# The opening of an S4-gated LoRA feed-forward kernel put in another order: adapter loads, adapter products, normalisation and the first chain

## Chip, core, metric

The kernel runs on one core of one Trainium2 chip. The metric is the device time in microseconds of one launch. Three runs of the kernel before took 466.06, 466.60 and 467.17 us, so its median is 466.6 us. Everything is float32.

## The reference, cut to what matters

```python
x  = u                                   # (2, 1024, 512): 2048 tokens of 512
xn = layernorm(x)                        # (x - mean) / sqrt(var + 1e-5), no gain, no bias
s  = fft_convolution(xn, K) + D * xn     # K: an S4 kernel of length 512, along the last axis
def lora(x, w, a, b):                    # rank 16, scaling 2
    return x @ w.T + 2.0 * (x @ a.T) @ b.T
h1 = lora(xn, w1, A1, B1)                # 512 -> 1376
h3 = lora(xn, w3, A3, B3)
f  = lora(silu(h1) * h3, w2, A2, B2)     # 1376 -> 512
out = x + s * silu(f)
```

The inputs w1 and w3 are 1376 x 512 each. 1376 is ten chunks of 128 and a last chunk of 96.

## The kernel before, in words

**Tiling.** The 2048 tokens are four blocks of 512 (b = 0 to 3), each held as four tiles of 128 tokens (`x_in[b][tt]`). A block is loaded (`load_x`), its mean and variance are taken (`norm_stats` on VectorE, or `act_sums`, `act_means`, `act_squares`, `act_variances` on ScalarE and GpSimd), the inverse root is found on VectorE by an integer guess and Newton steps (`norm_root`, `newton_rsqrt`), the tiles are scaled and shifted (`normalize`), turned by TensorE (`transpose`, 16 small matmuls per block) and copied from PSUM by ScalarE into `xr` (and `b12` for the odd blocks).

**Merging the adapters.** A weight tile gets its adapter added before use: TensorE forms B A into a PSUM bank (`lora_product`, 16 rows deep) and VectorE adds twice that to the tile (`merge`, L374). `merge_pair(c, w, half)` does so for one half of the 512 inputs of both w1 and w3 for a pair of chunks c; `lora_last` and `merge_last` do so for the chunk of 96. The adapter factors lie in two tiles, `lo_d` (A1, A3) and `lo_h` (B1, B3); their columns are in two halves, cut at 768 of 1376, and `load_lora(factors, queue, (half,))` loads one half with four transfers. Half 1 holds the last chunk, half 0 the first six chunks.

**Products.** The large product is a two-level Winograd scheme: sums of tokens (`outer_token_sum`, then `inner_token_sum`) and of weights (`outer_weight_sums`, `inner_weight_sum`) on VectorE, seven products per level on TensorE. One `Chain` is seven steps named 1, 2, 6, 7, 5, 3, 4 that go into PSUM banks x, w and y. After step 1 ScalarE copies x to w (L747); after steps 6 and 5 it saves x (`snapshot`, L729); sums with y (`total`, L733) are made on VectorE, gating is on ScalarE and GpSimd. The chain of the last chunk (`last_chain`) works at the outer level alone with four passes a step; each pair of chunks has seven chains (`pair_chain`) with two passes a step. The text calls step 1 of the last chunk "last P1", and so on.

**Order.** The order within TensorE, VectorE, ScalarE and GpSimd is written out by hand. Code that runs straight through comes first; then a heap of events, `at(place, what)`, is emptied in order of place, and each engine works through its own part in that order. Places are labels of order, not times. SyncE (SP) issues nearly all loads in program order; ScalarE's queue issues the adapter loads at the start. Eight semaphores go round among all loads of both queues, so a ninth load is issued only when an older one has landed.

**The opening.** SP loads block 0 (four transfers of 256 KB), block 1, the last chunk (`load_last`), pair 0 (`load_pair`), blocks 2 and 3, and pair 1. TensorE runs 24 idle matmuls on `ident` (`keep_warm`, two passes each), `lora_last`, then between more idle ones the transposes of block 0, and last P1. The two weight halves of pair 0 are merged at the places -9 and -3.8, the statistics of block 2 are taken from place -6 on, and the token sums of blocks 0 and 1 begin at place -2.3.

```python
    at(-9, lambda: merge_pair(0, w_pair[0], 0))
    at(-3.8, lambda: merge_pair(0, w_pair[0], 1))
    for i in range(2):
        at(-6 + i, lambda i=i: transpose(1, range(2 * i, 2 * i + 2), "y"))
    for tt in range(NTT):
        at(-6 + 0.8 * tt, lambda tt=tt: norm_stats(2, (tt,)))
```

Of the kernel before, what the change touches and what calls it, by code (L numbers as in the profile page):

```python
# [34 lines left out]

A_AT = {1: 0, 2: 1, 3: 6, 4: 2, 5: 3, 6: 4, 7: 5}
# [5 lines left out]

def newton_rsqrt(nc, pool, v, shape):

    y = pool.tile(shape, F32, tag="rs_y", name="rs_y")
    t = pool.tile(shape, F32, tag="rs_t", name="rs_t")
    nc.vector.tensor_scalar(
        y.bitcast(I32), v.bitcast(I32), -0.5, float(0x5F3759DF), ALU.mult, ALU.add  # L50
    )
    for _ in range(3):
        nc.vector.tensor_tensor(t, y, y, ALU.mult)
        nc.vector.scalar_tensor_tensor(t, t, -0.5, v, ALU.mult, ALU.mult)
        nc.vector.scalar_tensor_tensor(y, t, 1.5, y, ALU.add, ALU.mult)
    return y
# [40 lines left out]
def s4_gated_ffn(  # L97
# [106 lines left out]
    def after(delay, what):  # L204
        at(now[0] + delay, what)
# [4 lines left out]
    def load_x(b):  # L210
        room = (None, None, t_in[4], t_in[6])[b]
        tiles = []
        for tt in range(NTT):
            t = value() if room is None else room[:, tt, :]
            nc.sync.dma_start(out=t, in_=x[bass.ds(b * TB + tt * P, P), :])
            tiles.append(t)
        return tiles
# [17 lines left out]
    def act_sums(b, tt):  # L235
        if tt == 0:
# [5 lines left out]
    def act_means(b):  # L242
        sums = sums_of_x[b]
        nc.gpsimd.tensor_scalar(sums[:, 1, :], sums[:, 0, :], -1.0 / DIM, None, mult)
        nc.gpsimd.tensor_scalar(norms[b][:, :, 0], sums[:, 0, :], 1.0 / DIM, None, mult)

# [9 lines left out]

    def act_variances(b):
        nc.gpsimd.tensor_scalar(
            norms[b][:, :, 1], sums_of_x[b][:, 2, :], 1.0 / DIM, None, mult
        )  # L260

    def norm_root(mv, *blocks):
        n = len(blocks) * NTT
        veps = small.tile([P, n], F32, tag="veps", name="veps")
        nc.vector.tensor_scalar(veps, mv[:, :, 1], EPS, None, add)
        rstd = newton_rsqrt(nc, small, veps, [P, n])
        shift = small.tile([P, n], F32, tag="shift", name="shift")
        nc.vector.scalar_tensor_tensor(shift, mv[:, :, 0], -1.0, rstd, mult, mult)
# [3 lines left out]
    def normalize(b, on_act=(0, 2)):  # L272
        rstd, shift = norms[b]
        for tt, t in enumerate(x_in[b]):
            one = slice(tt, tt + 1)
            if tt in on_act:
                nc.scalar.activation(
                    t, t, AF.Identity, bias=shift[:, one], scale=rstd[:, one]
                )
            else:  # L280
                nc.gpsimd.tensor_scalar(t, t, rstd[:, one], shift[:, one], mult, add)

# [18 lines left out]
    def outer_token_sum(sb, name):  # L301
        b11, b21, b22 = (xr[:, i, sb] for i in range(3))
        t = [xt[:, i, sb] for i in range(4)]
        one, other = {
            1: (b12[sb], b11),
            2: (t[2], b11),
            3: (b22, b12[sb]),
            4: (b21, t[1]),
        }[name]
        nc.vector.tensor_tensor(t[name - 1], one, other, add if name == 2 else sub)  # L310

# [65 lines left out]
    def load_pair(c):  # L377
        w = wpool.tile([P, 8, 2, 2, P], F32, tag="w", name="w")
        for v, src in enumerate((w1T, w3T)):
            for half in range(2):  # L380
                slot = (1, 2, 0, 3)[2 * v + half]
                rows = src[half * HALF : (half + 1) * HALF, 2 * c * P : 2 * (c + 1) * P]
# [6 lines left out]
    def merge_pair(c, w, half, tag="aux"):  # L389

        ps = [bank(tag), bank(tag)]
        for k in range(2):
            for v in range(2):
                n = slice(k * 2 * P, (k + 1) * 2 * P)
                lora_product(ps[v][:, n], v, 2 * half + k, 2 * c * P, 2 * P, k == 0)
        for v in range(2):
            to = w[:, (1, 2, 0, 3)[2 * v + half]].rearrange("p k m h -> p (k m h)")
            after(1.6 + v, lambda to=to, v=v: merge(to, ps[v]))

# [66 lines left out]
    def load_w2():  # L466
        lora_tiles()
        load_lora(((b2T, a2),), nc.sync, (0, 1))
        w2["a"] = wpool.tile([P, 8, DIM], F32, tag="w", name="w2_a")
        w2["b"] = const.tile([P, 3, DIM], F32, tag="w2b", name="w2_b")  # L470
        nc.sync.dma_start(
            out=w2["a"], in_=w2T[: 8 * P, :].rearrange("(c p) d -> p c d", p=P)
        )
        nc.sync.dma_start(
            out=w2["b"][:, :2], in_=w2T[8 * P : LAST * P, :].rearrange("(c p) d -> p c d", p=P)
        )
        nc.sync.dma_start(out=w2["b"][:LASTR, 2], in_=w2T[LAST * P :, :])
# [4 lines left out]
    def merge_down(*chunks):  # L482

        made = []
        for fc in chunks:
            rows = P if fc < LAST else LASTR
            ps = aux()[:rows, :]
            d, h = lora_factors(0, 1, fc * P, rows)
            nc.tensor.matmul(ps, lhsT=h, rhs=d, start=True, stop=True)  # L489
# [216 lines left out]

    def product(ps, pairs, first):
        for i, (lhsT, rhs) in enumerate(pairs):
            nc.tensor.matmul(  # L709
                ps,  # L710
                lhsT=lhsT,
                rhs=rhs,
                start=first and i == 0,
                stop=i == len(pairs) - 1,
                skip_group_check=True,
            )


    class Chain:

        def __init__(self, pairs, rows, keep, got, late=0):
            self.pairs, self.rows, self.keep, self.got = pairs, rows, keep, got
            self.late = late

# [9 lines left out]
        def step(self, i):  # L736
# [6 lines left out]
            to = self.w if i == 2 else self.y if i in (7, 4) else self.x  # L743
            product(to, self.pairs(i), i in (1, 7))
            if i == 1:
# [47 lines left out]
    def last_chain(ab, sb):  # L793
# [12 lines left out]

        return Chain(pairs, LASTR, lambda o: value(), got, 1)

# [104 lines left out]
    lora_tiles()  # L913
    factors = (a1, b1T), (a3, b3T)
    load_lora(factors, nc.scalar, (1,))
    nc.scalar.activation(warm, warm, AF.Silu)
    load_lora(factors, nc.scalar, (0,))
    x_in[1] = load_x(1)
# [3 lines left out]
    x_in[2], x_in[3] = load_x(2), load_x(3)  # L922
    w_pair[1] = load_pair(1)

    def keep_warm(ps, n, first=False):
# [11 lines left out]
    for ps in primed:  # L937
        keep_warm(ps, 12, True)
    ps_last = lora_last()
    mv = norm_tile(0)  # L940
    norm_stats(0, range(NTT))
    norm_root(mv, 0)
    normalize(0)

    for i in range(2):
        keep_warm(primed[1], (5, 2)[i])
        transpose(0, range(2 * i, 2 * i + 2))
    keep_warm(primed[1], 4)
    mv = norm_tile(1)
    norm_stats(1, range(2))  # L950
    merge_last(w_last, ps_last, 0)
    norm_stats(1, range(2, NTT))
    norm_root(mv, 1)
    merge_last(w_last, ps_last, 1)
    mv_late = norm_tile(2, 3)
# [13 lines left out]
    for c in range(NPAIR):  # L969
# [6 lines left out]
        lambda: last_chain(ab_last, 0),  # L976
        ((1, -11), (2, -8), (7, -2), (6, 1.6), (5, 5.6), (3, 8.6), (4, 11.6)),
    )
    add_chain(
        0,  # L980
        pair_chain(0, 0),
        ((1, -4), (2, -1.8), (7, 3.6), (6, 4.6), (5, 7.6), (3, 10.6), (4, 13.6)),
    )
# [4 lines left out]
    for c in range(1, NPAIR):  # L988
        for n in range(7):

            hurry = (c, n) in ((NPAIR - 2, 6), (NPAIR - 1, 4))
            add_chain(2 + 7 * c + n, pair_chain(c, n), SOON if hurry else PLACES)
    at(-10, lambda: normalize(1))
    at(-9.9, lambda: last_sums(w_last, s_last))
    at(-9, lambda: merge_pair(0, w_pair[0], 0))
    at(-3.8, lambda: merge_pair(0, w_pair[0], 1))
    for i in range(2):
        at(-6 + i, lambda i=i: transpose(1, range(2 * i, 2 * i + 2), "y"))
    for n, name in enumerate((3, 2, 1)):
# [469 lines left out]
```

## Time and profile before

| | before |
|---|---|
| median of three runs | 466.6 us (466.06 to 467.17) |
| the profiled execution, its own time | 465.92 us |
| span of its profile, first to last instruction | 464.1 us |
| granted TensorE clock over the span | 1.00 |
| TensorE busy | 451.9 us, 97% of the span, 1682 matmuls |
| VectorE busy | 290.3 us, 63% |
| ScalarE busy | 136.3 us, 29% |
| GpSimd busy | 194.4 us, 42% |
| DMA | 53.36 MB, 115 GB/s on average |

The profiled execution's own time is 1.8 us above its span; what lies around the span is not shown by the profile. All times below are from the start of the span. A float32 matmul is recorded as two passes, a transpose as one. In the timeline, a row gives the start, the length, the engine, the line, the operation, what is written from what, and in brackets the idle time ahead of it with what ended it. "SPq" and "ACTq" are the queues from which SyncE and ScalarE issue transfers.

### The profile page before, as it was taken

The numbers are of one execution on the slowest core, as the hardware profiler recorded it, in microseconds if no ns is written. First come the engines' busy times: TensorE is split into PE (matmuls) and PEld (weight loads), VectorE is DVE, ScalarE is ACT, GpSimd is POOL, SyncE is SP. The second block draws the span as 40 slices with busy tenths as digits, with TensorE's granted clock in tenths as the row PEclk, the third lists the DMA queues.
The fourth block names the chain that finished last, engine by engine and source line by source line (L and its number), as shares of the span: only waits on it lengthen the run. The fifth ranks groups of instructions, "written<-read, shape, count | busy, mean of one in ns | idle before, by whom it ended". The sixth has DMA issues, their size and how long they took to land.

```text
span 464.1 us, 5003 instructions
## 1 busy us (share of the span) xinstructions
PE 451.9 (97%) x1682; PEld 274.9 (59%) x1682; DVE 290.3 (63%) x494; ACT 136.3 (29%) x281; POOL 194.4 (42%) x156
## 2 busy tenths in 40 slices
PE   8999898989999999999999999999999999999996
PEld 8635333334433443344333344888889898999895
DVE  5898979664776477547745586959786123442222
ACT  2675242433234334432442133111111101111110
POOL 2324262497559555945693359500000112222221
PEclk9999999999999999999999999999999999999999
DMA  8910312015102410241036229296901842422211
GB/s 249 359 43 18 130 57 84 0 54 174 46 23 69 137 45 23 69 151 44 23 98 220 80 83 269 91 333 214 347 1 47 287 139 91 137 90 92 80 57 45
DMA packets 35049, 53.36 MB, mean 115 GB/s; under 512 B 4528, under 2 KB 21168, under 8 KB 34896
## 3 DMA queue, kind: packets, MB, share of 16 engines
q1 hardware_dynamic: 34768, 52.74, 34.6%
q10 hardware_dynamic: 256, 0.31, 0.2%
q8 instruction: 13, 0.21, 0.2%
q14 instruction: 12, 0.10, 0.1%
HBM read 33.64 MB, written 19.40 MB: 114 GB/s over the span
## 4 chain that ended last, share of the span: by engine, by line
PE 83%; DVE 8%; DMA 3%; ACT 2%; POOL 2%; issue 1%; SPq 0%; POOLq 0%
PE x L709 39%; PE y L709 21%; PE w L709 11%; PE aux L881 6%; PE aux L364 2%; PE aux L489 2%; DMA room<-g_dram 2%; DVE s L419 1%; DMA s<-in_x_dram 1%; DVE xt L310 1%; DVE s L733 1%; DVE w L407 1%; DVE t_in L326 1%; POOL s L790 1%; PE w L881 1%
## 5 line engine op out<-in xcount | busy, mean ns | idle before, releaser
L1236 POOL TENSOR_TENSOR o<-o,xin 128x512 f32<-128x512 f32 (+1 forms) x17 | 22.5, 1324 | 140.1 <-DVE o L1235 140.1
L790 POOL TENSOR_TENSOR s<-c,s 128x512 f32<-128x512 f32 (+1 forms) x44 | 59.6, 1356 | 23.2 <-ACT c L782 20.7
L729 ACT COPY s<-x 128x512 f32<-128x512 f32 (+1 forms) x54 | 31.6, 586 | 95.4 <-PE x L709 95.2
L709 PE MATMUL x<-t_in,s 128*128 128x512 f32 (+1 forms) x148 | 56.5, 504 | 0.0
L733 DVE TENSOR_TENSOR s<-s,y 128x512 f32<-128x512 f32 (+1 forms) x54 | 36.5, 681 | 24.1 <-PE y L709 14.4
L823 POOL TENSOR_TENSOR ua_three<-ua_three,s 128x512 f32<-128x512 f32 x20 | 29.8, 1489 | 34.9 <-DVE s L733 34.9
L709 PEld LDWEIGHTS x<-t_in,s 128*128 128x128 f32 x148 | 26.4, 189 | 21.8 <-issue 13.8
L823 POOL TENSOR_TENSOR s<-ua_three,s 128x512 f32<-128x512 f32 x18 | 29.8, 1653 | 21.5 <-DVE s L733 21.5
L709 PE MATMUL y<-t_in,s 128*128 128x256 f32 (+1 forms) x108 | 36.2, 461 | 1.4 <-DVE s L733 1.4
L1257 ACT COPY z<-x 128x256 f32<-128x256 f32 x24 | 8.9, 373 | 83.5 <-PE x L709 83.5
L782 ACT ACTIVATE c<-c 128x512 f32<-128x512 f32 x40 | 25.1, 632 | 12.7 <-DVE c L823 12.7
L709 PEld LDWEIGHTS y<-t_in,s 128*128 128x128 f32 x108 | 20.0, 190 | 13.4 <-issue 8.5
L823 POOL TENSOR_TENSOR s<-u_three,s 128x512 f32<-128x512 f32 x20 | 26.6, 1332 | 0.8
L747 ACT COPY w<-x 128x512 f32<-128x512 f32 (+1 forms) x37 | 21.5, 581 | 8.5 <-PE x L709 8.5
L881 PE MATMUL aux<-conv,xr 128*128 128x128 f32 (+1 forms) x128 | 23.2, 314 | 0.0
L709 PE MATMUL x<-xt,w 128*128 128x512 f32 x40 | 21.0, 607 | 0.7 <-ACT w L747 0.7
L709 PE MATMUL x<-t_in,w 128*128 128x512 f32 x40 | 21.3, 613 | 0.4 <-ACT w L747 0.4
L823 POOL TENSOR_TENSOR u_three<-ua_three,u_three 128x512 f32<-128x512 f32 x10 | 13.3, 1326 | 19.8 <-DVE u_three L733 17.9
L709 PE MATMUL x<-xr,w 128*128 128x512 f32 x40 | 20.8, 615 | 0.6 <-ACT ua_three L729 0.5
L1234 DVE TENSOR_TENSOR aux<-aux,m 128x256 f32<-128x256 f32 x16 | 6.9, 431 | 23.1 <-PE aux L881 23.1
L709 PE MATMUL x<-xr,s 128*128 128x512 f32 x40 | 20.6, 614 | 0.7 <-ACT s L729 0.7
L709 PE MATMUL y<-xt,w 128*128 128x512 f32 x40 | 19.9, 595 | 1.4 <-DVE s L733 1.4
(271 smaller groups left out, 871.5 us busy)
## 6 DMA issues: line engine op xcount, KB each, us to landing
g_dram<-s SPq DMA_DIRECT2D x40, 256.0 KB, 2.1
g<-g_dram SPq DMA_DIRECT2D x10, 512.0 KB, 5.7
xin<-in_x_dram SPq DMA_DIRECT2D x16, 256.0 KB, 2.7
out_dram<-o SPq DMA_DIRECT2D x14, 256.0 KB, 2.0
t_in<-g_dram SPq DMA_DIRECT2D x6, 512.0 KB, 4.2
w<-in_w1T_dram SPq DMA_DIRECT2D x10, 256.0 KB, 3.6
w<-in_w3T_dram SPq DMA_DIRECT2D x10, 256.0 KB, 4.4
s<-in_x_dram SPq DMA_DIRECT2D x8, 256.0 KB, 4.2
```

The lines of the kernel that those rows point to most:

```text
L364: nc.tensor.matmul(ps, lhsT=d[:, dc * P : (dc + 1) * P], rhs=h, start=start, stop=True, skip_group_check=True,)
L489: nc.tensor.matmul(ps, lhsT=h, rhs=d, start=True, stop=True)
L709: nc.tensor.matmul(ps, lhsT=lhsT, rhs=rhs, start=first and i == 0, stop=i == len(pairs) - 1, skip_group_check=True,)
L729: nc.scalar.copy(t, self.x)
L733: nc.vector.tensor_tensor(t, t, self.y, add)
L747: nc.scalar.copy(self.w, self.x)
L782: nc.scalar.activation(c, c if src is None else src, AF.Silu)
L790: nc.gpsimd.tensor_tensor(g, act, g, mult)
L823: (nc.vector if o < 20 else nc.gpsimd).tensor_tensor(to, a, b, add)
L881: nc.tensor.matmul(to, lhsT=x_, rhs=by, start=start, stop=True, skip_group_check=True)
L1236: (nc.vector if last else nc.gpsimd).tensor_tensor(o, o, self.xin[h][:, cols], add)
L1257: nc.scalar.copy(t, xb)
```

## The change

It has these parts:

1. ScalarE runs its first activation (the table load) ahead of the adapter loads instead of between them; adapter half 0 moves from ScalarE's queue to the end of SP's, behind pair 1. The chunks of the weights are walked in another order (`PAIR_AT`: columns 768, 1024, 0, 256, 512), so that pairs 0 and 1 need half 1, which is the half loaded first.
2. The adapter products of pair 0's first half are made right behind `lora_last`, ahead of block 0's transposes; 12 idle matmuls instead of 24 stand in front, 4 instead of 11 around the transposes.
3. Tile 1 of block 0 has its statistics on ScalarE and GpSimd (`act_tile`). The root takes ten instructions of VectorE, `veps` and `shift` among them, instead of twelve. Tile 0 of block 0 is normalised on VectorE instead of ScalarE.
4. Last P1 of blocks 0 and 1 is made in two halves of 256 tokens.
5. The places of the opening move: both halves of pair 0 are merged, and pair 0's chain 1 has its steps 1 and 2, ahead of or between block 1's transposes; the statistics of block 2 move from before the token sums to between and behind them; two of the four squares of block 3 move behind a snapshot.
6. The outer token sums are made in two instructions of 128x512 instead of one of 128x1024.
7. Blocks 2 and 3 are loaded with four transfers of 512 KB instead of eight of 256 KB; w2 is loaded with one transfer more.

```diff
+PAIR_AT = [2 * P * ((c + 3) % NPAIR) for c in range(NPAIR)]
+CHUNK_AT = [PAIR_AT[fc // 2] + fc % 2 * P for fc in range(LAST)] + [LAST * P]
...
-def newton_rsqrt(nc, pool, v, shape):
+def rsqrt(nc, pool, v, shape):
...
-    for _ in range(3):
-        nc.vector.tensor_tensor(t, y, y, ALU.mult)
-        nc.vector.scalar_tensor_tensor(t, t, -0.5, v, ALU.mult, ALU.mult)
-        nc.vector.scalar_tensor_tensor(y, t, 1.5, y, ALU.add, ALU.mult)
+    nc.vector.tensor_tensor(t, y, y, ALU.mult)
+    nc.vector.scalar_tensor_tensor(t, t, -c2, v, ALU.mult, ALU.mult)
+    nc.vector.scalar_tensor_tensor(y, t, c2 * 2.38924456, y, ALU.add, ALU.mult)
+    nc.vector.tensor_tensor(t, y, y, ALU.mult)
+    nc.vector.scalar_tensor_tensor(t, t, 1.0 / part**2, v, ALU.mult, ALU.mult)
+    nc.vector.scalar_tensor_tensor(t, t, -10.0 / 3.0, t, ALU.add, ALU.mult)
+    nc.vector.scalar_tensor_tensor(y, t, 5.0, y, ALU.add, ALU.mult)
...
+    def act_tile(b, tt):
+        one = slice(tt, tt + 1)
+        act_sums(b, tt)
+        act_means(b, one)
+        act_squares(b, tt)
+        act_variances(b, one)
...
-        nc.vector.tensor_tensor(t[name - 1], one, other, add if name == 2 else sub)
+        for k in range(2):
+            to, a, b = (v[:, k] for v in (t[name - 1], one, other))
+            nc.vector.tensor_tensor(to, a, b, add if name == 2 else sub)
...
-            product(to, self.pairs(i), i in (1, 7))
+            product(to, self.pairs(i), i in (1, 7), self.parts if i == 1 else 1)
...
+    nc.scalar.activation(warm, warm, AF.Silu)
     load_lora(factors, nc.scalar, (1,))
-    nc.scalar.activation(warm, warm, AF.Silu)
-    load_lora(factors, nc.scalar, (0,))
...
     w_pair[1] = load_pair(1)
+    load_lora(factors, nc.sync, (0,))
...
     for ps in primed:
-        keep_warm(ps, 12, True)
+        keep_warm(ps, 6, True)
     ps_last = lora_last()
+    merge_pair(0, w_pair[0], 0, ("x", "w"), (-10.6, -10.5))
     mv = norm_tile(0)
-    norm_stats(0, range(NTT))
+    act_tile(0, 1)
+    norm_stats(0, (0, 2, 3))
     norm_root(mv, 0)
-    normalize(0)
-
-    for i in range(2):
-        keep_warm(primed[1], (5, 2)[i])
-        transpose(0, range(2 * i, 2 * i + 2))
+    mv = norm_tile(1)
+    normalize(0, (2,), (0,))
     keep_warm(primed[1], 4)
-    mv = norm_tile(1)
+    transpose(0, range(NTT))
     norm_stats(1, range(2))
     merge_last(w_last, ps_last, 0)
     norm_stats(1, range(2, NTT))
-    norm_root(mv, 1)
-    merge_last(w_last, ps_last, 1)
...
-        ((1, -11), (2, -8), (7, -2), (6, 1.6), (5, 5.6), (3, 8.6), (4, 11.6)),
+        ((1, -11), (2, -10), (7, -2), (6, 1.6), (5, 5.6), (3, 8.6), (4, 11.6)),
...
-        ((1, -4), (2, -1.8), (7, 3.6), (6, 4.6), (5, 7.6), (3, 10.6), (4, 13.6)),
+        ((1, -8.7), (2, -6), (7, 3.6), (6, 4.6), (5, 7.6), (3, 10.6), (4, 13.6)),
...
-    at(-10, lambda: normalize(1))
-    at(-9.9, lambda: last_sums(w_last, s_last))
-    at(-9, lambda: merge_pair(0, w_pair[0], 0))
-    at(-3.8, lambda: merge_pair(0, w_pair[0], 1))
+    at(-10.9, lambda: norm_root(mv, 1))
+    at(-10.8, lambda: normalize(1))
+    at(-10.7, lambda: merge_last(w_last, ps_last, 1))
+    at(-10.6, lambda: last_sums(w_last, s_last))
+    at(-10.4, lambda: merge_pair(0, w_pair[0], 1, places=(-9.9, -9.8)))
     for i in range(2):
-        at(-6 + i, lambda i=i: transpose(1, range(2 * i, 2 * i + 2), "y"))
+        at(-9 + 0.5 * i, lambda i=i: transpose(1, range(2 * i, 2 * i + 2), "y"))
...
-        at(-6 + 0.8 * tt, lambda tt=tt: norm_stats(2, (tt,)))
+        at((-1.4, 0.2, 1, 1.1)[tt], lambda tt=tt: norm_stats(2, (tt,)))
...
-        at(-0.3 + 0.1 * tt, lambda tt=tt: act_squares(3, tt))
+        at((-0.3, -0.2, 1.7, 1.8)[tt], lambda tt=tt: act_squares(3, tt))
...
-    at(0.2, lambda: act_variances(3))
+    at(1.9, lambda: act_variances(3))
```

More of the change, by code (lines that the diff above doesn't have):

```diff
@@ L42 @@
 SOON = ((1, 0), (6, 3), (2, 4), (7, 5), (5, 6), (3, 9), (4, 11))
-def newton_rsqrt(nc, pool, v, shape):
+def rsqrt(nc, pool, v, shape):
     y = pool.tile(shape, F32, tag="rs_y", name="rs_y")
     t = pool.tile(shape, F32, tag="rs_t", name="rs_t")
+    part = 3.0 / 8.0
+    c2 = part * 0.703952253
     nc.vector.tensor_scalar(
-        y.bitcast(I32), v.bitcast(I32), -0.5, float(0x5F3759DF), ALU.mult, ALU.add
+        y.bitcast(I32), v.bitcast(I32), -0.5, float(0x5F1FFFF9), ALU.mult, ALU.add
     )
-    for _ in range(3):
-        nc.vector.tensor_tensor(t, y, y, ALU.mult)
-        nc.vector.scalar_tensor_tensor(t, t, -0.5, v, ALU.mult, ALU.mult)
-        nc.vector.scalar_tensor_tensor(y, t, 1.5, y, ALU.add, ALU.mult)
+    nc.vector.tensor_tensor(t, y, y, ALU.mult)
[5 more added lines that the diff above has]
+    nc.vector.scalar_tensor_tensor(y, t, 5.0, y, ALU.add, ALU.mult)
     return y
@@ L210, in load_x @@
     def load_x(b):
[L211 to L216, printed above, removed]
+        room, tiles = (None, None, t_in[4], t_in[6])[b], []
+        n = 1 if room is None else 2
+        for tt in range(0, NTT, n):
+            to = value().unsqueeze(1) if room is None else room[:, tt : tt + n, :]
+            rows = x[bass.ds(b * TB + tt * P, n * P), :]
+            nc.sync.dma_start(out=to, in_=rows.rearrange("(k p) d -> p k d", p=P))
+            tiles += [to[:, k, :] for k in range(n)]
         return tiles
@@ L235, in act_sums @@
     def act_sums(b, tt):
-        if tt == 0:
+        if b not in sums_of_x:
             sums_of_x[b] = small.tile([P, 3, NTT], F32, tag="act_sums", name="act_sums")
@@ L240, in act_sums, with act_means @@
         )
[L242 to L245, printed above, removed]
+    def act_means(b, tiles=slice(0, NTT)):
+        s, neg, _ = (sums_of_x[b][:, i, tiles] for i in range(3))
+        nc.gpsimd.tensor_scalar(neg, s, -1.0 / DIM, None, mult)
+        nc.gpsimd.tensor_scalar(norms[b][:, tiles, 0], s, 1.0 / DIM, None, mult)
     def act_squares(b, tt):
@@ L255, in act_squares, with act_variances @@
         )
-    def act_variances(b):
+    def act_variances(b, tiles=slice(0, NTT)):
         nc.gpsimd.tensor_scalar(
-            norms[b][:, :, 1], sums_of_x[b][:, 2, :], 1.0 / DIM, None, mult
+            norms[b][:, tiles, 1], sums_of_x[b][:, 2, tiles], 1.0 / DIM, None, mult
         )
+    def act_tile(b, tt):
[4 more added lines that the diff above has]
+        act_variances(b, one)
     def norm_root(mv, *blocks):
@@ L265, in norm_root @@
         nc.vector.tensor_scalar(veps, mv[:, :, 1], EPS, None, add)
-        rstd = newton_rsqrt(nc, small, veps, [P, n])
+        rstd = rsqrt(nc, small, veps, [P, n])
         shift = small.tile([P, n], F32, tag="shift", name="shift")
@@ L270, in norm_root, with normalize @@
             norms[b] = [t[:, n * NTT : (n + 1) * NTT] for t in (rstd, shift)]
-    def normalize(b, on_act=(0, 2)):
+    def normalize(b, on_act=(0, 2), on_vector=()):
         rstd, shift = norms[b]
@@ L280, in normalize @@
             else:
-                nc.gpsimd.tensor_scalar(t, t, rstd[:, one], shift[:, one], mult, add)
+                engine = nc.vector if tt in on_vector else nc.gpsimd
+                engine.tensor_scalar(t, t, rstd[:, one], shift[:, one], mult, add)
     def transpose(b, tiles, tag="aux"):
@@ L381, in load_pair @@
                 slot = (1, 2, 0, 3)[2 * v + half]
-                rows = src[half * HALF : (half + 1) * HALF, 2 * c * P : 2 * (c + 1) * P]
+                rows = src[half * HALF : (half + 1) * HALF, PAIR_AT[c] : PAIR_AT[c] + 2 * P]
                 nc.sync.dma_start(
@@ L387, in load_pair, with merge_pair @@
         return w
-    def merge_pair(c, w, half, tag="aux"):
-        ps = [bank(tag), bank(tag)]
+    def merge_pair(c, w, half, tags=("aux", "aux"), places=None):
+        ps = [bank(tag) for tag in tags]
         for k in range(2):
@@ L394, in merge_pair @@
                 n = slice(k * 2 * P, (k + 1) * 2 * P)
-                lora_product(ps[v][:, n], v, 2 * half + k, 2 * c * P, 2 * P, k == 0)
+                lora_product(ps[v][:, n], v, 2 * half + k, PAIR_AT[c], 2 * P, k == 0)
         for v in range(2):
             to = w[:, (1, 2, 0, 3)[2 * v + half]].rearrange("p k m h -> p (k m h)")
-            after(1.6 + v, lambda to=to, v=v: merge(to, ps[v]))
+            when = places[v] if places else now[0] + 1.6 + v
+            at(when, lambda to=to, v=v: merge(to, ps[v]))
     def outer_weight_sums(w, names):
@@ L470, in load_w2 @@
         w2["b"] = const.tile([P, 3, DIM], F32, tag="w2b", name="w2_b")
[L471 to L476, printed above, removed]
+        for c in range(0, LAST, 4):
+            to = w2["a"][:, c : c + 4] if c < 8 else w2["b"][:, :2]
+            n = to.shape[1] * P
+            rows = w2T[CHUNK_AT[c] : CHUNK_AT[c] + n, :]
+            nc.sync.dma_start(out=to, in_=rows.rearrange("(c p) d -> p c d", p=P))
         nc.sync.dma_start(out=w2["b"][:LASTR, 2], in_=w2T[LAST * P :, :])
@@ L487, in merge_down @@
             ps = aux()[:rows, :]
-            d, h = lora_factors(0, 1, fc * P, rows)
+            d, h = lora_factors(0, 1, CHUNK_AT[fc], rows)
             nc.tensor.matmul(ps, lhsT=h, rhs=d, start=True, stop=True)
@@ L704, in s4_matrix, with product, __init__ @@
         yield
[L707 to L716, printed above, removed]
+    def product(ps, pairs, first, parts=1):
+        n = ps.shape[1] // parts
+        for part in range(parts):
+            cols = slice(part * n, (part + 1) * n)
+            for i, (lhsT, rhs) in enumerate(pairs):
+                nc.tensor.matmul(
+                    ps[:, cols],
+                    lhsT=lhsT,
+                    rhs=rhs if parts == 1 else rhs[:, cols],
+                    start=first and i == 0 and part == 0,
+                    stop=i == len(pairs) - 1,
+                    skip_group_check=True,
+                )
     class Chain:
-        def __init__(self, pairs, rows, keep, got, late=0):
+        def __init__(self, pairs, rows, keep, got, late=0, parts=1):
             self.pairs, self.rows, self.keep, self.got = pairs, rows, keep, got
-            self.late = late
+            self.late, self.parts = late, parts
         def snapshot(self, o):
@@ L805, in got @@
                 gate.put(o, c)
-        return Chain(pairs, LASTR, lambda o: value(), got, 1)
+        return Chain(pairs, LASTR, lambda o: value(), got, 1, 2 if sb == 0 else 1)
     def pair_chains(c, w, s, order):
```

## The prediction

> **What bounds the kernel now.** I read the page first, then the chain of waits in order of time, the timeline of the first 56 us, the busy time by stretch, and the landing of each load.
>
> ```profile
> span 464.1 us, 5003 instructions
> PE 451.9 (97%) x1682; PEld 274.9 (59%) x1682; DVE 290.3 (63%) x494; ACT 136.3 (29%) x281; POOL 194.4 (42%) x156
> ...
> PE   8999898989999999999999999999999999999996
> ...
> DVE  5898979664776477547745586959786123442222
> ```
>
> TensorE is full nearly everywhere, so time comes off at the opening. But VectorE's second to sixth slices stand at 8, 9, 8, 9, 7. The chain shows who leads where:
>
> ```profile
> 2.10 4.69 DMA s<-in_x_dram
> ...
> 9.93 0.17 DVE shift L268
> ...
> 10.99 1.09 PE aux L288 x8
> ...
> 14.42 1.74 PE x L709 x4
> 16.16 1.06 PE aux L364 x8
> 17.23 1.89 PE w L709 x4
> ...
> 37.92 0.68 DVE w L374
> 38.60 1.01 DVE s L419
> ...
> 53.81 0.61 DVE s L733
> ...
> 54.47 1.13 PE y L709 x2
> ```
>
> Block 0's load, the statistics and the root lead to 10.1, TensorE leads on to 37, and from 37.9 to 54.4 VectorE does, mostly.
>
> ```profile
> 40.00:50.00 10.00, 10.00 (x49) 5.99 (x48) 9.93 (x12) 7.21 (x17) 3.56 (x2) 1.00 0.40 136
> 50.00:60.00 10.00, 8.64 (x21) 3.12 (x20) 10.00 (x8) 1.14 (x2) 3.25 (x1) 1.00 0.10 36
> ...
> 22.23 1.22 DVE L310 TENSOR_TENSOR xt<-xr,b 128x1024 f32<-128x1024 f32 x1 [0.49 <-ACT xr L299]
> ...
> 37.31 1.29 DVE L374 SCALAR_TENSOR_TENSOR w<-aux,w 128x512 f32<-128x512 f32 x2 [0.87 <-PE aux L364]
> ...
> 54.47 1.13 PE L709 MATMUL y<-xt,w 128*128 128x512 f32 x2 [1.36 <-DVE s L733]
> ```
>
> Columns of the first two rows: TensorE, weight loads, VectorE, ScalarE, GpSimd. VectorE runs without a pause from 37.31 to 54.41, and TensorE then waits 1.36 us for it. So what counts is not when TensorE starts but when VectorE reaches 54.41; from there TensorE runs on to 68.5 and everything later follows it. I work out two times: S, the first transpose of block 0 (10.99 before), and X, the first outer token sum (22.23 before).
>
> **S: loads, adapter products, root.** Loads land in order of issue, whichever queue issued them. Block 0's tiles, issued at 0.72, 1.16, 1.63 and 2.10, took 2.9, 3.7, 4.2 and 4.7; the four of adapter half 1, at 0.71, 1.17, 1.63 and 2.10, took 2.5, 3.9, 3.7 and 4.6; block 1's first, at 3.24, took 4.2 and landed at 7.4, its second at 8.2, its third at 9.3. Afterwards the adapter loads stand behind the table load (1.28 us in the trace, 2.58 to 3.86). No row shows whether a transfer on ScalarE's queue waits for a table load ahead of it: from nothing to 1.5 us (load plus the 0.20 activation). And only eight loads are open: the adapter's last is likely the ninth or tenth, so it waits for block 0's first or second tile (3.6 to 4.6). In order of issue it then lands just behind block 1's first tile, 7.45, or second, 8.2. Bounds for that landing, L: 6.8 (nothing lost) and 9.5 (all four behind block 1). I take 7.45, the nearest row for a load issued at 3.2 to 3.7.
>
> [...] the adapter load of 5.32 took 4.3 us and landed at 9.6, behind a block 1 tile issued at 5.08 that took 4.2. I take the rows.
>
> Behind L, TensorE works in order: `lora_last` 1.06 (8.47 to 9.53), four products 1.07 (16.09 to 17.16), four idle matmuls 0.90 (eight passes by 0.112). S = L + 3.03 = 10.5. The other limit: block 0's last tile lands at 6.6 to 6.8 (some adapter traffic gone from in front of it), statistics 0.94, root ten times 0.20 = 1.98 (twelve took 7.75 to 10.09), so `shift` ends near 9.6; VectorE's scaling of tile 0 is 0.48 by its nearest row (L533, 128x512), 0.77 at most (GpSimd's for the same): 10.1 to 10.4. ScalarE's tile: landed 4.8, sum 0.84, means 0.5 on an idle GpSimd (it waited 8.36 us for `shift`), squares 0.91, variance 0.25: 7.4, hidden beside tile 3. If the adapter load ahead of it on ScalarE's queue waits for block 0's last tile, it isn't.
>
> [...] In the trace 14 passes fit in 1.4 to 4.4 and 29 in 5 to 8, so a cold start is real. TensorE would now idle from 5.9 to L = 7.45. The row for an idle spell is 1.36 us at 54.47, after which passes take the usual 0.43: cost nothing. [...] cold, the 3.03 doubles and S is 3 us later. I take nothing and keep 3 us for the range.
>
> **From S to X.** Four transposed tiles with ScalarE's copies (0.54 each, two banks): S+2.27. Last P1 in halves is 8 passes of about 0.215 for 4 of 0.43, no gain in itself; its first half can start while the copies of tiles 2 and 3 run. P1 ends S+4.05; products of half 1 1.07; P2 1.79; transposes of block 1 0.89; pair P1 0.90; transposes 0.89; the rest of ScalarE's copies about 1.0. X = S + 10.65 = 21.15, against 22.23. Along the way: `merge_last` ends near 12.1 on VectorE, before P1; block 1's root is ten instructions behind four statistics, 15.6 instead of 16.1, and its tiles are scaled by 16.5 and 17.2, under TensorE's S+6.9 = 17.4. VectorE then makes five merges until 18.7 and waits for X; that wait held block 2's statistics before (18.46 to 21.74).
>
> **From X to 54.41 on VectorE.** Before, 22.23 to 38.51 (first L419): 16.28. Taken out: idle 0.47 + 0.40 + 0.87 = 1.74 (VectorE is late, so TensorE and ScalarE are ready); two merges of half 1, now ahead of X, 1.21; root 0.40. Added: four statistics by 0.80 = 3.20; each token sum is two of about 0.61 (L407's spacing) for one of 1.13, +0.08, four times 0.32. Sum 16.45. Then block 1's four sums +0.32 to 54.41. The shift is 22.23 + 16.28 - X - 16.45 - 0.32 = 21.74 - X = 11.09 - S = **0.6 us earlier** for S = 10.5. TensorE itself reaches last P7 at about 21.8 instead of 23.60, but gives that back: pair P7 waits for the weight sum at X+5.1, the products of pair 1's half 1 for PSUM banks that VectorE frees at X+13.9.
>
> Costed at nothing: adapter half 0 on SP behind pair 1 (four issues of 0.43 after 19.9, ahead of a spill that waits for copies until 21.95; first needed by pair 2, far on, else that merge waits); blocks 2 and 3 in four transfers (needed after X, landed by 19 to 22 before; late, VectorE waits at the first statistics); GpSimd's three small instructions; ScalarE's two squares behind a snapshot (1.4 us sooner for the snapshot, TensorE's 0.63 wait at 30.45; the variance is needed only at X+10.7); the order of chunks; w2 in one transfer more (TensorE has no wait between 105 and 286). Without these covers each costs under 1 us.
>
> The profiled execution took 465.92 (464.1 and 1.8 around): 465.3 by the sum. It lies 0.7 below the median of 466.6, which gives 466.0.
>
> **Rivals.**
> - *TensorE's start carries through.* If VectorE has more slack than I count, or L is at its low bound, last P7's 1.8 us comes through whole, 464.8, or 2.3 at S = 10, 464.3. For: all of TensorE's slices are full. Against: the 1.36 us wait at 54.47 ends on VectorE.
> - *The adapter comes late.* Its last load holds TensorE's queue, and with it block 0's transposes. It decides from S = 11.09, that is L = 8.06, and each microsecond beyond is one lost: L = 9 gives +0.9, 467.5; L = 9.5 gives +1.4, 468.0, and a cold clock up to 3 us more. For: eight semaphores, landing in order of issue. Against: the loads are small, and only the last has to wait.
> - *It doesn't do what it says*: the two cancel and the time stays within 0.93 us (0.2%, about what a measurement of this kernel can tell from no change). My likeliest case lies in it.
>
> **How the numbers follow.** My case, 466.0, own range 465.2 to 466.8: 40% (32 of it same, 8 faster). TensorE's start carries through: 37% (34 faster, 3 same). Adapter late: 23% (20 slower, 3 same). Faster 0.42, same 0.38, slower 0.20. The range of 464.3 to 467.6 takes in the first rival whole and the second up to L = 9, and leaves out a late adapter with a cold clock and gains over 2.3.
>
> **What would show it.** `lora_last` at 7.5 (8.47 before), block 0's first transpose at 10.5, last P1 at 12.8 (14.26 before), the first token sum at 21.2, `shift` of blocks 2 and 3 near 33.8 (32.98 before: later), the first L419 near 37.6, TensorE's wait before y<-xt,w grown over 1.36 with its end near 53.9. Wrong if `lora_last` starts after 8.1, if VectorE pauses between X and 54, or if the wait at 54.47 shrinks.

## The result, and the profile after

The changed kernel takes 473.1 us (471.05, 473.05, 473.14 and 473.38), against 466.33 for the kernel before: a ratio of 1.0131, 95% interval 1.0108 to 1.0155. It is slower by 6.8 us, where 0.6 faster was forecast with a range up to 467.6. The profiled execution took 471.05 us, the shortest of the four; what the others lost beyond it no profile shows.

The page of the changed kernel; after the span, the busy shares by fortieths of the span, and the granted clock of TensorE in tenths:

```profile
span 469.3 us, 4955 instructions
...
PE   7989999899999999999999999999999999999996
...
DVE  5578988675777476647765685969797123542222
...
PEclk9798999999999999999999999999999999999999
```

The clock row has a 7 in the second slice and an 8 in the fourth. The busy rows do not show it: block 0's 16 transposes take 3.51 us at half clock, 0.22 each, where four of block 1's took 0.45 before, 0.11 each, and TensorE is recorded as busy all the while. The busy time by stretch of the changed kernel shows it sharply; the columns are TensorE, weight loads, VectorE, ScalarE, GpSimd, granted clock, DMA share, GB/s:

```profile
7.16:10.58 3.42, 1.49 (x21) 1.30 (x22) 2.92 (x14) 0.83 (x2) 0.94 (x2) 1.00 1.13 308
10.58:13.99 3.41, 3.41 (x16) 2.66 (x13) 3.27 (x9) 0.01 (x1) 1.06 (x2) 0.50 1.09 348
13.99:17.40 3.41, 3.41 (x18) 3.04 (x17) 3.07 (x14) 1.76 (x3) 1.31 (x2) 0.50 1.05 387
...
37.88:41.30 3.42, 2.38 (x11) 1.01 (x9) 2.36 (x7) 2.69 (x4) 2.73 (x4) 1.00 0.00 0
41.30:44.71 3.41, 3.41 (x4) 1.29 (x5) 3.38 (x5) 0.58 (x1) 1.04 (x2) 0.50 0.00 0
```

The clock in this profile is either 1.00 or 0.50, and its changes while TensorE works, at 10.58, 17.40, 41.30 and 44.71, lie whole multiples of 3.41 us apart (two, seven and one). Three such stretches run at half: two in the opening, which hold block 0's transposes, and one at 41 us. The first and the third follow a stretch in which TensorE was recorded busy for 1.49 and 2.38 of 3.42 us, and all 1.49 and 1.73 of that were adapter products, 16 rows deep. The second follows the first, which began with such products too, 1.42 of its 3.41 us.

The chain of waits in order of time names what led up to them:

```profile
1.16 3.75 DMA s<-in_x_dram
...
4.93 4.37 DMA lo_h<-in_b3T_dram
...
9.34 1.01 PE y L386 x13
...
12.00 2.00 PE w L953 x8
14.00 3.51 PE aux L308 x16
17.52 1.78 PE x L735 x8
...
25.74 2.50 DVE xt L332 x4
...
38.50 2.22 ACT t_in L296 x3
40.73 0.48 ACT ua_three L755
41.20 0.04 issue
41.25 2.06 PE x L735 x2
```

The adapter's last load, issued at 4.93, lands at 9.30; before, `lora_last` began at 8.47. Then eight passes on `ident` take 2.0 us, and block 0's transposes start at 13.8 and run until 17.5. The first outer token sum is at 25.74, 3.5 later than before. Near 40 us ScalarE scales three tiles of blocks 2 and 3 as soon as VectorE has their root (`shift` ends at 38.48), and only then saves `ua_three`, for which TensorE and VectorE both wait. In the timeline, VectorE's two waits, and the wait that stood at 54.47 before:

```profile
41.23 0.69 DVE L759 TENSOR_TENSOR ua_three<-ua_three,y 128x512 f32<-128x512 f32 x1 [0.97 <-ACT ua_three L755]
...
45.82 0.68 DVE L759 TENSOR_TENSOR s<-s,y 96x512 f32<-96x512 f32 x1 [0.58 <-PE y L735]
...
59.92 1.12 PE L735 MATMUL y<-xt,w 128*128 128x512 f32 x2 [1.07 <-DVE s L759]
```

The last is 5.45 later than before, and the rest follows: the span is 5.2 longer.

### The profile page after: what moved, and what is told of

The parts are those of the page before. It is cut to its first block, busy times and chain, and to the rows that moved or that the text cites. A ratio compares the mean times of both kernels' runs of the same rounds, so it can differ in the third digit from the quotient of the medians.

```text
span 469.3 us, 4955 instructions
## 1 busy us (share of the span) xinstructions
PE 454.1 (97%) x1648; PEld 275.8 (59%) x1648; DVE 289.2 (62%) x495; ACT 137.1 (29%) x284; POOL 196.9 (42%) x159
## 4 chain that ended last, share of the span: by engine, by line
PE 83%; DVE 8%; DMA 4%; ACT 2%; POOL 2%; issue 1%; SPq 0%; POOLq 0%; DVEq 0%
PE x L735 38%; PE y L735 21%; PE w L735 11%; PE aux L907 6%; DVE xt L332 2%; PE aux L512 2%; PE aux L386 2%; DMA room<-g_dram 1%; PE aux L308 1%; DMA lo_h<-in_b3T_dram 1%; DVE t_in L348 1%; POOL s L816 1%; DVE s L759 1%; DMA s<-in_x_dram 1%; PE w L907 1%
## 5 line engine op out<-in xcount | busy, mean ns | idle before, releaser
L849 POOL TENSOR_TENSOR s<-ua_three,s 128x512 f32<-128x512 f32 x18 | 31.4, 1745 | 22.0 <-DVE s L759 22.0
L735 PE MATMUL x<-xr,w 128*128 128x512 f32 x40 | 21.8, 639 | 1.0 <-ACT ua_three L755 0.9
```

Of the source, the lines that this page charges most:

```text
L735: nc.tensor.matmul(ps[:, cols], lhsT=lhsT, rhs=rhs if parts == 1 else rhs[:, cols], start=first and i == 0 and part == 0, stop=i == len(pa ...
L849: (nc.vector if o < 20 else nc.gpsimd).tensor_tensor(to, a, b, add)
```

## Experiments

The runs of one kernel differ in how many stretches at half clock they caught, so I give two numbers: the median of all runs with its ratio to the kernel before, and the median of the runs whose granted clock over the span was 0.998 or more (called "whole"; the clock is recorded for each run). "Whole" has a blind spot: the record reads 1.00 until its first change, so it does not tell how long a run was at half at its very start. The kernel before has whole medians of 466.4, 466.3 and 466.0 us in the three sets (94 of 123 runs), and 467.7 to 468.0 at a clock of 0.994 to 0.996. One stretch of 3.41 us at half takes about 0.004 off the mean clock (half of 3.41 in 466), so by that sum these runs are one stretch apart, and it costs about 1.6 us (1.4 to 1.7 in the three sets).

**Is it the clock, or VectorE's load?** My theory was that the late adapter load leaves TensorE idle, and that the clock falls for it. The rival was that block 2's statistics, moved into VectorE's long stretch, are the whole loss. First, more idle matmuls:

```diff
-        keep_warm(ps, 6, True)
+        keep_warm(ps, 14, True)
```

> The changed kernel with 28 idle matmuls on TensorE ahead of the adapter products instead of 12; the adapter's last load still lands at about 9.3. Theory (the late adapter leaves TensorE idle, and the clock drops to half): the clock stays whole through the opening, the first transpose of block 0 comes at about 12.4 instead of 13.8, the first token sum at about 23.1 instead of 25.7, and the time is about 467.6 us, 1.3 above before: what is left is the wait for the adapter alone. Rival (VectorE has too much to do between the token sums and 54 us): nothing changes, 472 to 473 us.

Measured: 470.21 us, ratio 1.0066 (1.0028 to 1.0104). Better by 2.9, not by 5.5. In its profile the opening is at a whole clock from the adapter products on (four transposes in 0.45 us), but the 56 passes ended only at 10.23: they took 8.86 us, where 56 of 0.11 would take 6.2. That delayed the adapter products by 0.9. The stretch near 40 us stays, and there is another at 262 us. The row ahead of the one near 40 us shows how short the gaps were there, 0.52 us in all:

```profile
37.03:40.44 3.41, 2.89 (x11) 1.59 (x12) 2.44 (x5) 2.19 (x5) 3.34 (x5) 1.00 0.00 0
```

Here TensorE is recorded busy for 2.89 of 3.41 us, and the clock still fell at 40.44. The passes in it include the eight adapter products of pair 1, which are 16 rows deep and recorded as busy for 1.73 us of it.

Second, the adapter loads ahead of the activation, as before:

```diff
-    nc.scalar.activation(warm, warm, AF.Silu)
     load_lora(factors, nc.scalar, (1,))
+    nc.scalar.activation(warm, warm, AF.Silu)
```

> The changed kernel with the adapter loads of half 1 issued ahead of ScalarE's first activation, as before the change; all else stays. Theory: adapter products start at about 6.8 instead of 9.3, first transpose of block 0 at about 10.1, first token sum at about 20.8, no half clock in the opening, 465.4 us (0.9 below before), or 467 if the second half-clock window, at 41 us, stays. Rival (VectorE's load): 471 to 473 us.

Measured: 469.04 us, 1.0049 (1.0027 to 1.0071). The adapter products start at 6.9 as expected, but the time is 3.6 above the 465.4 that I expected, and 2.0 above the 467 that I gave for the case that the later stretch at half stays, as it does (38.93 to 42.35). My theory fell here in its first form: without the late load the clock of the opening falls all the same.

```profile
4.80:8.21 3.41, 2.81 (x31) 2.56 (x32) 2.03 (x7) 1.53 (x4) 0.62 (x3) 1.00 1.05 338
8.21:11.62 3.41, 3.41 (x17) 2.72 (x14) 3.03 (x14) 0.81 (x1) 1.40 (x2) 0.50 1.14 320
```

The longest gap in the first stretch is 0.6 us, yet the second is at half. What the stretch holds are adapter products: those of the last chunk and those of pair 0, which the change put one behind the other.

Third, those two parts alone in the kernel before (the activation first, 12 idle matmuls):

```diff
+    nc.scalar.activation(warm, warm, AF.Silu)
     load_lora(factors, nc.scalar, (1,))
-    nc.scalar.activation(warm, warm, AF.Silu)
     load_lora(factors, nc.scalar, (0,))
...
-        keep_warm(ps, 12, True)
+        keep_warm(ps, 6, True)
```

> The kernel before with two parts of the change alone: ScalarE's first activation ahead of its adapter loads, and 12 idle matmuls instead of 24. Theory: adapter products at 8.5 to 9.5, TensorE idle ahead of them from about 6, at least one half-clock window, 468.5 to 470.5 us. Rival (VectorE's load, which is as before here): 466.3 to 467.3 us.

Measured: 469.80 us, 1.0058 (1.0040 to 1.0077), adapter products at 9.2, half clock from 10.24 to 13.66 in the profile (ten passes on `ident` in 2.43 us). The rival would leave this kernel at 466.3 to 467.3, so VectorE's load isn't needed for a loss of 3 us. But it may add to it. Fourth, e2_adapter_first with block 2's statistics back:

```diff
-        at((-1.4, 0.2, 1, 1.1)[tt], lambda tt=tt: norm_stats(2, (tt,)))
+        at(-6 + 0.8 * tt, lambda tt=tt: norm_stats(2, (tt,)))
```

> As e2_adapter_first, and the statistics of block 2 back at their places before the token sums. Theory: VectorE takes them while it would wait for the transposes of block 1 (18.7 to 20.8), so its long stretch up to the wait at 54 us starts 1 us later but is 3.2 us shorter: about 2 us below e2_adapter_first, 463.4 us. Rival (VectorE's load is the whole cause): e2_adapter_first is slow and this one makes good most of it, 467 us.

Measured: 464.89 us, 0.9961 (0.9948 to 0.9974); its three whole runs have a median of 464.1. So the statistics matter as well: 4.1 below e2_adapter_first, more than the 2 of VectorE's time. In the profile the half-clock stretch at 39 us is gone too. So is the one in the opening (the clock over the span is 1.00), but this profile is of the shortest of the 20 runs, and 17 of them did lose some clock, so how the 4.1 divides is not shown.

**Which passes go ahead of half clock?** e5_mixed is e2_adapter_first with idle matmuls of 128 rows between the two groups of adapter products:

```diff
     ps_last = lora_last()
+    keep_warm(primed[1], 5)
...
-    keep_warm(primed[1], 4)
+    keep_warm(primed[1], 2)
     transpose(0, range(NTT))
```

> As e2_adapter_first, with five idle matmuls put between the last chunk's adapter products and those of pair 0 and two instead of four ahead of block 0's transposes. In e2_adapter_first the clock fell to half at 8.2 after a stretch of 3.4 us in which TensorE was recorded busy for 2.8. Theory (products 16 rows deep hardly count as activity[...]): with idle matmuls of 128 rows between them the clock stays whole in most runs until 39 us, and the time is 466 to 467 us, 2 to 3 below e2_adapter_first. Rival (the clock falls for any gap, and what costs time is VectorE): 469 us as e2_adapter_first.

Measured: 467.73 us, 1.0018 (0.9999 to 1.0038); whole: 465.77 (two runs of 20). It is 1.3 below e2_adapter_first, not 2 to 3: the opening keeps its clock in the profile (eight transposes in 1.06 us at 11.05), and the stretch at 38 us doesn't (0.50 from 38.01 to 41.42). Those two whole runs are what my sum was for: 0.5 below the kernel before's 466.3. The edit has three idle matmuls more than e2_adapter_first, so by itself it does not part their depth from their number.

This profile has one more stretch at half, at 260 us, where 16-row products for w2 stand (L512). The stretch ahead of it, whole and then for L512 alone, and the stretch at half:

```profile
256.45:259.86 3.41, 3.41 (x10) 1.09 (x10) 2.12 (x4) 1.16 (x2) 3.33 (x3) 1.00 0.00 0
...
256.45:259.86 3.41, 2.42 (x8) 0.79 (x8) 1.00 0.00 0
...
259.86:263.28 3.42, 3.42 (x5) 1.18 (x4) 1.42 (x3) 0.00 (x0) 0.34 (x1) 0.50 0.27 81
```

TensorE is recorded as busy without any gap, 2.42 of the 3.41 us with 16-row products, and the clock falls. The profiles of e1_idle28 and e9_before_rows16 have the same at 262.3 and 264.7 us (3.41 busy, 2.32 and 2.40 of it 16 rows deep). So the recorded busy time did not decide here, though some waiting may be in it: the last four of these passes are recorded at 1.81 us, for 1.13 elsewhere. In the kernel before, the stretch from 8.05 to 11.47 us holds 1.13 of 16-row products beside 2.2 of full-depth passes, and its clock stays whole.

e6_mixed_stats has both edits, e5's and e4's.

> As e4_stats_early with the same idle matmuls as e5_mixed: theory 463.5 us, 1.4 below e4_stats_early, whose runs lay between 463.6 at a whole clock and 467.6 at 0.991. Rival: no change from e4_stats_early, 464.9.

Measured: 463.51 us, 0.9946 (0.9918 to 0.9973), whole 463.51, in five runs. This version beats both kernels. Its timeline:

```profile
6.76 1.13 PE L386 MATMUL y<-lo_h,lo_d 16*128 16x96 f32 x16
7.82 1.38 PE L953 MATMUL w<-ident 128*128 128x128 f32 x10
...
10.20 0.71 PE L953 MATMUL w<-ident 128*128 128x128 f32 x4
10.74 1.04 PE L308 MATMUL aux<-ident,s 128*128 128x128 f32 x8
...
22.07 1.26 DVE L332 TENSOR_TENSOR xt<-xr,b 128x512 f32<-128x512 f32 x2
...
52.40 1.13 PE L735 MATMUL y<-xt,w 128*128 128x512 f32 x2 [1.51 <-DVE s L759]
```

The transposes start at 10.74 instead of 13.8, at 0.11 us a pass instead of 0.22; the wait ends at 52.40, 2.1 ahead of the kernel before.

e7_after_stats is the changed kernel with e4's edit alone, the adapter still late.

> The changed kernel with block 2's statistics back at their places before the token sums, the adapter still late. Theory: the half-clock window at 41 us goes, since TensorE no longer waits for VectorE there, and VectorE's stretch is shorter by about 2; the half clock in the opening stays: 469 us, 4 below the changed kernel. Rival (the late adapter and the opening's clock are all of it): 472 to 473 us.

Measured: 468.35 us, 1.0041 (1.0027 to 1.0054), as expected and 4.75 below the changed kernel. In its profile the half clock goes from 7.87 to 18.11 and there is none near 40 us: the statistics cause the one at 41 us, the opening the rest. The other profiles agree: those with the statistics moved (the changed kernel, e1, e2, e5) all have a stretch at half near 40 us, and those with the statistics at their old places have none: the clock over the span is 0.999 or 1.00 in the kernel before, e4, e6, e8, e11 and e12, and what e3, e7, e9 and e10 lost lies in the opening or at 264.7. From the first token sum to the end of TensorE's wait, VectorE takes 34.18 us in the changed kernel (25.74 to 59.92) and 30.36 here (26.44 to 56.80).

e8_before_nofill takes the idle matmuls around block 0's transposes out of the kernel before:

```diff
-        keep_warm(primed[1], (5, 2)[i])
...
-    keep_warm(primed[1], 4)
```

> The kernel before without the eleven idle matmuls around block 0's transposes; they compute nothing that is used, and the 24 ahead of the adapter products stay. Theory: the stretch from 8 to 11.5 us has the 16-row products and little else, the clock falls to half for one or two windows, 468 to 469.5 us though TensorE has less to do. Rival (idle matmuls are only in the way): transposes up to 0.5 us earlier, 466 us.

Measured: 467.55 us, 1.0026 (1.0009 to 1.0043). Whole: 466.58, but in only 9 of 20 runs, where the kernel before has 94 of 123; six runs at 0.991 to 0.992 have 468.87. So the average moves the way of the theory, by less than its 468 to 469.5, and not in every run. The steps of 3.41 us start elsewhere in each profile (changes at 7.87, 8.21, 10.24 and 10.58 us in e7, e2, e3 and the changed kernel). That the idle matmuls make half clock rarer fits these counts; how they do it is not shown.

The disputed cost by itself is e9_before_rows16: the kernel before, its first 24 idle matmuls 16 rows deep.

```diff
-                lhsT=ident,
-                rhs=ident,
+                lhsT=ident[:rows, :],
+                rhs=ident[:rows, :],
...
-        keep_warm(ps, 12, True)
+        keep_warm(ps, 12, True, R)
```

> The kernel before, its 24 idle matmuls at the start made 16 rows deep instead of 128; they compute nothing that is used, and TensorE is as busy by the record. Theory (passes 16 rows deep hardly count as activity): the clock, which became whole at 4.6 us before, stays at half past 8 us at least, the adapter products and block 0's transposes run at half, and the time is 468 to 470 us. Rival (any busy TensorE keeps the clock): whole at about 4.6 as before, 466.4 us.

Measured: 472.50 us, 1.0117 (1.0083 to 1.0152). The timeline of TensorE has no gap:

```profile
1.37 9.97 PE L927 MATMUL w<-ident 16*128 16x128 f32 x45 [1.37 <-POOL ident masks.py:199]
...
12.88 2.50 PE L927 MATMUL w<-ident 128*128 128x128 f32 x10
15.17 1.91 PE L288 MATMUL aux<-ident,s 128*128 128x128 f32 x8
...
19.18 1.06 PE L927 MATMUL w<-ident 128*128 128x128 f32 x8
```

48 passes at 0.21 us each last past 10.9. Ten passes on `ident` then take 2.50 us, for 1.38 in the kernel before. Only at 18.90 does the clock become whole, 14 us later than before (4.64), though TensorE is recorded as busy throughout (3.41 of the 3.41 us from 15.49 to 18.90). These passes of 16 rows did not raise the clock. The time is above the 468 to 470 expected. Some 2.4 of the 6.2 us lost are these passes themselves, which hold back the adapter products (10.92 for 8.47).

**The other terms of the sum.** e12_late_filled is e6_mixed_stats with the adapter loads late and 24 idle matmuls:

```diff
+    nc.scalar.activation(warm, warm, AF.Silu)
     load_lora(factors, nc.scalar, (1,))
-    nc.scalar.activation(warm, warm, AF.Silu)
...
-        keep_warm(ps, 6, True)
+        keep_warm(ps, 12, True)
```

> As e6_mixed_stats, but the adapter loads late again, behind ScalarE's first activation, and 24 idle matmuls instead of 12 in the time of waiting. It parts the lateness from the clock. Theory: adapter products at 9.3, first transpose at about 13, first token sum at about 23.6 instead of 22.1, clock whole: 465.0 us, 1.5 above e6_mixed_stats. Rival (the clock was all of the loss): 463.5.

Measured: 465.78 us, 0.9990 (0.9979 to 1.0002); whole 465.69 in 14 of 20 runs. So with a whole clock the lateness costs 2.2 us against e6_mixed_stats, for the 1.5 expected. That is at most: the idle matmuls end at 9.79, 0.3 after the adapter has landed at 9.46.

```profile
9.72 1.13 PE L386 MATMUL y<-lo_h,lo_d 16*128 16x96 f32 x16
...
13.71 1.04 PE L308 MATMUL aux<-ident,s 128*128 128x128 f32 x8
...
24.37 1.29 DVE L332 TENSOR_TENSOR xt<-xr,b 128x512 f32<-128x512 f32 x2 [0.86 <-ACT xr L319]
```

e10_sums_whole is e6_mixed_stats with each outer token sum in one instruction.

```diff
-        for k in range(2):
-            to, a, b = (v[:, k] for v in (t[name - 1], one, other))
-            nc.vector.tensor_tensor(to, a, b, add if name == 2 else sub)
+        nc.vector.tensor_tensor(t[name - 1], one, other, add if name == 2 else sub)
```

> As e6_mixed_stats with the outer token sums in one instruction each, as before the change. The prediction put the split at 0.08 us a sum, eight sums, 0.64 us on VectorE's long stretch. Theory: 0.3 to 0.6 us below e6_mixed_stats, 463.0. Rival (the split lets the seventh step of the last chain start 0.6 us sooner, and that counts): 0.5 above, 464.0.

Measured: 465.60 us, 0.9980 (0.9959 to 1.0002); whole 463.70 in three runs. Against e6_mixed_stats' whole 463.51 there is nothing to tell in these few runs: neither the 0.3 to 0.6 below nor the 0.5 above. But the profile, of a run of 468.32, is at half from 7.97 to 18.2 us, with the same opening as e6_mixed_stats. So the idle matmuls between the products do not keep the clock in every run, and the 463.51 of e6_mixed_stats' five runs may be a lucky median.

e11_p1_whole is e6_mixed_stats with last P1 in one piece.

```diff
-        return Chain(pairs, LASTR, lambda o: value(), got, 1, 2 if sb == 0 else 1)
+        return Chain(pairs, LASTR, lambda o: value(), got, 1, 1)
```

> As e6_mixed_stats with step 1 of the last chain in one piece. It then waits for ScalarE's copies of all four tiles of block 0, about 0.8 us longer. Theory (VectorE is busy with block 2's statistics then, and sets the first token sum): no difference, 463.5. Rival (TensorE sets the pace there): 0.6 to 0.8 slower, 464.2.

Measured: 464.14 us, 0.9963 (0.9942 to 0.9985); whole 463.95 in 11 of 15 runs, 0.4 above e6_mixed_stats' three. The products behind P1 come 0.9 later (15.77 for 14.89), the first token sum only 0.2 (22.29 for 22.07). Between the two expectations, and with few runs to compare it stays open.

## Why the prediction was wrong, by its steps

Three steps failed. The sum had the end of TensorE's wait 0.6 earlier than before, and it came 5.45 later. In the sum's own terms the difference of 6.05 is L 1.85 (9.30 for 7.45), L to S 1.47 (4.50 for 3.03), S to X 1.29 (11.94 for 10.65), and X to the wait's end 1.45 (34.18, where 32.24 before with 0.17 and 0.32 more makes 32.73).

**The landing of the adapter's last load, L.** I took 7.45 and it was 9.30. I had it issued at 3.2 to 3.7 as the ninth or tenth load; it was the eleventh, issued at 4.93, when block 0's second tile landed (4.9); eight were open by 2.58, and the ninth went out at 3.8, when the first tile had landed (3.8). The prediction names that tile but misreads its row: issued at 1.16 and landing after 3.7, it landed at 4.9 in the kernel before too, not at 4.6. Block 1's third tile had been issued by then, at 4.22, on the landing of the adapter's own first load (4.1), and so stood ahead of it. The row I chose, landing in order of issue, was right: the load took 4.4 us and landed behind that tile. The table load cost nothing: the first adapter load was issued at 0.85, while the table load ran from 0.71 to 1.99. At a whole clock the lateness is worth up to 2.2 us (e12_late_filled against e6_mixed_stats).

**The clock, costed at nothing.** I weighed the idle spell by the gap in TensorE's work and gave it up to 3 us, only from L = 9, a bound that no trace had shown. The terms L to S and S to X came out 2.76 us over: TensorE had no gap over 1.93 us in the opening once it had begun, and yet the products, the transposes and the passes on `ident` ran at half from 10.58 to 17.40. Nor was a gap needed: in e5_mixed a stretch recorded as busy for all of its 3.41 us was followed by half. The row that I took for an idle spell, 1.36 us at 54.47, stands between passes of full depth and says nothing of 16-row products.

The change made stretches short of full-depth passes in three ways: 12 and seven idle matmuls fewer, two groups of 16-row products in a row, and the waits of TensorE near 40 us for VectorE's merge (0.64) and ScalarE's copy (0.40), again around 16-row products. Only the first two are in the opening. By subtraction, as an estimate: the change at a whole clock without the lateness is -0.5 (e5_mixed, whole), lateness +2.2, together 468 us; the other 5 us of 473.1 go with the clock, about three stretches of 1.6. That the clock follows the rows in use is my reading and not shown; shown is that 9.97 us of 16-row passes did not raise it (e9_before_rows16) and that it fell behind a stretch recorded as full, 2.42 of its 3.41 us with such passes (e5_mixed).

**VectorE without a pause from X on.** I took 1.74 us of idle time out of VectorE's stretch because it would be late and the others ready, and named a pause as a sign of being wrong. It paused for 1.55: 0.97 for ScalarE's copy of `ua_three`, queued behind the scaling that waits for VectorE's own root, and 0.58 for TensorE at half clock. The 0.97 is no matter of the clock: e6_mixed_stats and e12_late_filled have it too.

What held:

- S to X: I had 10.65. e5_mixed has 21.71 - 11.05 = 10.66, e12_late_filled 24.37 - 13.71 = 10.66.
- The total at a whole clock: two runs of e5_mixed came within 0.3 of the 466.0 forecast. This may be luck in part, as the pause of 0.97 was not in the sum and neither run has a profile. They are also all that speaks for the parts costed at nothing (the larger loads, the order of chunks, adapter half 0 behind pair 1), none of which was run alone.
- The moved statistics as a load on VectorE, 3.2 us: its stretch is 3.82 longer with them (34.18 for 30.36), 0.58 of it the wait for TensorE at half clock. Back in the idle stretch ahead of X they delay X by 0.67 only (e6_mixed_stats has 11.33 from S to X for 10.66), and e6_mixed_stats takes 463.5. I had named that idle time without drawing the conclusion that the move itself was a loss.
- The start of the root: `shift` ended at 9.7 for 9.6 forecast; VectorE's scaling of tile 0 took 0.55, between its two bounds.
- The split token sums: 0.08 each was too much. Block 1's four took 4.82 in the changed kernel (52.70 to 57.52) and 4.66 before, 0.04 each.

The second rival, the late adapter, is the larger part of what came, with L at 9.3 and a clock at half, and it was priced at 1.2 and up to 3 more for the latter. The range left that case out as too rare.

## What to carry to other kernels

Before taking filler matmuls out or putting shallow products (few rows of the array) in a row, lay the stretches between the recorded changes of the clock (steps of 3.41 us in these profiles) over TensorE's work and count what is full-depth in each: the busy share didn't tell here (3.41 of 3.41 us in e5_mixed, and half clock after it). The adapter's last load stood next on its queue behind one issued at 1.73 and went out only at 4.93, on a landing at 4.9, so list which landing releases each early load. And work moved "behind" the critical step on a busy engine should be set against the idle time that it leaves there.

## What the runs showed of the hardware that I had not expected

- Passes 16 rows deep, 45 of them back to back in 9.97 us (0.21 us each), left the clock at half; the 128-row passes after them ran at half for 6 us more, from 12.88 to 18.90 (e9_before_rows16).
- The granted clock in the profile reads 1.00 before its first recorded change even where passes take twice as long: in the kernel before 14 passes on `ident` lie between 1.4 and 4.4 us and 29 between 5 and 8, all at a reading of 1.00. In e9_before_rows16 it does so for 18.9 us:

```profile
1.83:5.25 3.42, 3.42 (x18) 3.42 (x18) 1.06 (x3) 1.49 (x2) 0.00 (x0) 1.00 0.97 274
```

- A transfer queued on ScalarE behind a table load was issued 0.14 us after that load began (0.85 and 0.71, the changed kernel).
